# A four-layer graph network: stationary weights in layer 0, row tables made in its loop, fixed order in layer 1, layer 2's tables beside layer 1's lists

## The chip, the cores and the metric

The kernel runs on one core of a Trainium2 chip. The metric is the device time in microseconds; lower is better. PE is the matrix engine (PEld its weight load), DVE the vector engine, ACT the engine of activation functions, POOL the general engine, which here issues the gathers, and SP the engine that issues plain transfers.

## The reference, cut to what matters

B = 8 batches, N = 2048 nodes, D = 64 features; `adj` is 2048 x 2048 with about eight edges a row. Four layers follow each other, each `x = layernorm(x + layer(x, adj))`:

```
layer 0: h = LN((x*nw + nb + x) @ W)
         e = leaky_relu(s1[:, :, None] + s2[:, None, :]); att = softmax(where(adj, e, -big))
         layer = elu(att @ h + h)
layer 1: feat = softplus(x*w0/sqrt(2) + b0); p = exp(feat*wa + ba)       (per feature)
         layer = (A @ (p*feat)) / (A @ p)
layer 2: layer = LN(relu(x @ W_self + b + (A @ x / deg) @ W_neigh + b'))
layer 3: four attention heads over adj, an output product, a second attention, LN
```

`A` is `adj > 0`. The factor `exp(ba)` falls out of layer 1's quotient.

## The kernel before

The nodes are 16 tiles (NT) of 128. A first stage reads `adj`, builds for each tile a list of its edges (five blocks of 128 list places for each of two groups of 64 nodes: GS = 5, NG = 2), the selection matrices `Sel`, `SelT`, and for the first DENSE = 8 tiles the transposed matrix `ET`. It also makes layer 0's `H` and its table `htab0` in DRAM.

A tile's neighbours can be summed in two ways. *By list*: ten gathers (`gather`, L204, an indirect transfer that POOL issues) fetch the neighbours' rows from a table in DRAM, one row per list place, and PE multiplies them by the selection matrices. *By matrix*: PE multiplies `ET` with the rows of all 16 tiles, which must be in SBUF, split into three bf16 pieces (`hi`, `mid`, `lo`).

Layer 0 (L435 to L535) is by list for all tiles, in an order written out by hand (`manual_schedule`: each engine gets its instructions in the order of the Python calls). Step k issues the gathers of tile k+1 (`fetch`), makes the edge weights of tile k (`weights`), divides tile k-1, combines tile k-2 with `H`, multiplies tile k's gathered rows by the weights on DVE and sums them on PE (`weigh`, L476 and L482), then activates tile k-2 and normalises tiles k-3.

Layer 1 (L543 to L692) first makes the rows `p` and `p*feat` of four tiles at a time (`make_rows`, L580 to L597), stores them in the table `rtab` and splits them into the pieces `R` for the matrix way; beside this PE sums matrix tiles 0 to 2 (`FIRST`). When the table is whole, the gathers for tiles 15 to 8 begin, three groups of list blocks a tile (`quads`; four, four and two gathers of 4 KB rows), spread between the steps of matrix tiles 3 to 7. `finish` (L614 to L617) divides and adds to `X`; each pair of tiles is then normalised. A scheduler sets the engines' order here.

Layer 2 (L776 to L1000) turns each tile of `X` and multiplies it by both weight matrices (L805 to L825), stores `ytab`, splits the product into `Y` and keeps `S`. Then, in a fixed order, steps of matrix tiles 0 to 7 and groups of list tiles 15 to 8 (`quads`) alternate; LATE and EARLY say how many matrix steps stand before the first and after the last group. `chain` normalises finished tiles, and `show` copies them on POOL (L908) and stores `xtab`, from which layer 3 gathers.

## Time and profile before

| | us |
|---|---|
| median of 9 runs | 1765.13 (1761.21 to 1769.31) |
| the profiled execution | 1767.85 |
| its span | 1765.7 |
| first gather of layer 0 | 186.1 |
| first weights of layer 0's loop (L461), last | 201.5, 401.1 |
| first gather of layer 1, of layer 2, of layer 3 | 530.8, 749.6, 923.2 |

The profile is one execution. A window's busy time tells how full an engine was in it, not which engine set the pace; the chain of waits and the idle time before an instruction tell that. Instructions of one engine that do not depend on each other overlap a little: DVE's products of 512 elements show 0.69 us each and start 0.60 us apart.

### The profile page before, as it was taken

To read this page: it belongs to the slowest core of one execution; us is meant where nothing else is said; L and a number is where in the kernel's file an instruction comes from. 1 tells how busy PE (TensorE), PEld (TensorE's weight loads), DVE (VectorE), ACT (ScalarE), POOL (GpSimd) and SP (SyncE) were. 2 spreads that over 40 slices of the span, in tenths; PEclk is the share of its full clock that TensorE was granted. 3 is DMA by queue.
4 is the path that set the end of the run, shared out by engine and by line. 5 is a ranking of instruction groups with operands and counts; after the bars stand their busy time and mean duration, and the time that the engine had idled before them with its cause. 6 is when DMAs were issued, how large, how long until landed. Compare 5 with 4: busy or idle time off the path is not lost.

```text
span 1765.7 us, 38671 instructions
## 1 busy us (share of the span) xinstructions
PE 1392.7 (79%) x15264; PEld 956.7 (54%) x15264; DVE 1198.3 (68%) x2931; ACT 932.0 (53%) x1943; POOL 870.8 (49%) x820
## 2 busy tenths in 40 slices
PE   4673354552789996898829999999999986999993
PEld 3663232331233333632217877777777775878783
DVE  5889479996666564765764666666666654787787
ACT  5763244545952232544655656656656533577674
POOL 0000577670665551666525454554554516677761
PEclk9655567666799998999968999999999987999997
DMA  6451576660226982266514555554555427687771
GB/s 187 164 173 42 167 202 192 190 200 17 95 96 241 329 309 87 95 177 187 168 51 124 146 143 141 154 154 130 154 150 155 137 69 228 180 234 219 211 214 45
DMA packets 154135, 280.64 MB, mean 159 GB/s; under 512 B 64892, under 2 KB 91452, under 8 KB 151868
## 3 DMA queue, kind: packets, MB, share of 16 engines
q0 software_dynamic: 56320, 189.44, 35.5%
q1 hardware_dynamic: 80986, 84.45, 16.3%
q10 hardware_dynamic: 16640, 4.20, 1.0%
q8 instruction: 123, 2.02, 0.5%
q14 instruction: 66, 0.54, 0.1%
HBM read 237.60 MB, written 40.42 MB: 157 GB/s over the span
## 4 chain that ended last, share of the span: by engine, by line
PE 43%; DVE 13%; ACT 6%; issue 4%; POOL 2%; DMA 1%; DVEq 0%; SPq 0%; ACTq 0%; POOLq 0%
PE pscore L1081 8%; PE pa L605 6%; PE po L1103 5%; PE pt L1068 4%; PE pscore L1044 4%; PE pa L660 3%; PE ps L1385 2%; PE po L1424 2%; PE py L812 2%; DVE z L1156 2%; PE pt L1362 1%; ACT z L849 1%; PE pa L982 1%; PE pscore L1166 1%; POOL hs L204 1%
## 5 line engine op out<-in xcount | busy, mean ns | idle before, releaser
L204 POOL DMA_INDIRECT hs<-htab,src x160 | 153.2, 957 | 240.4 <-PE pe L455 181.5
L204 POOL DMA_INDIRECT xs<-xtab,src x160 | 207.0, 1294 | 113.9 <-PE po L1103 63.9
L1087 DVE SCALAR_TENSOR_TENSOR w<-w,Sel 128x640 f32<-128x640 f32 (+2 forms) x160 | 153.3, 958 | 135.1 <-ACT w L1084 133.9
L605 PE MATMUL pa<-R,ET 128*128 128x512 bf16 x768 | 178.6, 389 | 51.6 <-POOL R L593 34.6
L204 POOL DMA_INDIRECT hs<-ktab,src x160 | 158.1, 988 | 61.8 <-issue 34.5
L1081 PE MATMUL pscore<-U,xsT 64*128 64x80 f32 (+2 forms) x2560 | 182.7, 282 | 0.0
L1081 PEld LDWEIGHTS pscore<-U,xsT 64*128 64x128 f32 x2560 | 157.5, 189 | 43.5 <-ACT xsT L1070 22.7
L170 ACT ACTIVATE X<-X,ln_m,ln_r 128x64 f32<-128x64 f32 x256 | 87.2, 428 | 144.8 <-DVE ln_m L162 144.8
L605 PEld LDWEIGHTS <-ET 128*128 128x128 fp8e4 x768 | 74.6, 100 | 163.5 <-issue 83.0
L1070 ACT COPY xsT<-pt 128x512 f32<-128x512 f32 x160 | 93.7, 586 | 103.6 <-PE pt L1068 103.6
L1084 ACT ACTIVATE w<-pscore 128x640 f32<-128x640 f32 (+2 forms) x160 | 119.6, 747 | 46.8 <-PE pscore L1081 44.9
L1103 PE MATMUL po<-w,xs 128*64 128x88 f32 (+2 forms) x3072 | 139.6, 237 | 0.7 <-DVE w L1087 0.7
L1068 PE MATMUL pt<-ident,xs 128*128 128x128 f32 x640 | 106.8, 290 | 33.9 <-DMA xs<-xtab,src 33.2
L1103 PEld LDWEIGHTS po<-w,xs 128*64 128x64 f32 x3072 | 114.0, 137 | 15.3 <-DVE w L1087 0.9
L204 POOL DMA_INDIRECT rs<-rtab,src x80 | 75.9, 949 | 62.7 <-PE pa L660 43.1
L614 DVE RECIPROCAL rec<-pa 128x256 f32<-128x256 f32 x32 | 54.2, 1731 | 64.3 <-PE pa L660 38.5
L1385 PE MATMUL ps<-U,hsT 128*128 128x64 f32 x768 | 95.5, 271 | 1.5 <-ACT hsT L1363 1.5
L1385 PEld LDWEIGHTS ps<-U,hsT 128*128 128x128 f32 x768 | 94.2, 195 | 1.9 <-ACT hsT L1363 1.7
L1068 PEld LDWEIGHTS pt<-ident,xs 128*128 128x128 f32 x640 | 68.3, 142 | 48.7 <-DMA xs<-xtab,src 33.4
L476 DVE TENSOR_TENSOR hs<-hs,w 128x1024 f32<-128x1024 f32 x80 | 91.9, 1214 | 3.2 <-ACT w L465 3.2
L1472 ACT ACTIVATE z<-z,ln_m,ln_r 128x64 f32<-128x64 f32 x240 | 83.5, 431 | 15.3 <-DVE ln_m L1460 15.3
L982 PE MATMUL pa<-Y,ET 128*128 128x512 bf16 x384 | 89.9, 383 | 0.0
(636 smaller groups left out, 3077.0 us busy)
## 6 DMA issues: line engine op xcount, KB each, us to landing
at<-in_adj SPq DMA_DIRECT2D x16, 1024.0 KB
R<-itab SPq DMA_DIRECT2D x60, 256.0 KB
rtab<-r SPq DMA_DIRECT2D x16, 512.0 KB
ptab<-hp SPq DMA_DIRECT2D x16, 384.0 KB
hi<-ptab SPq DMA_DIRECT2D x16, 384.0 KB
ktab<-hb SPq DMA_DIRECT2D x16, 260.0 KB
X<-in_x ACTq DMA_DIRECT2D x16, 256.0 KB
htab<-H SPq DMA_DIRECT2D x16, 256.0 KB
```

What stands on the lines that cost most here:

```text
L170: nc.scalar.activation(v[:, b], v[:, b], AF.Identity, scale=rstd[:, k:k + 1], bias=nmr[:, k:k + 1])
L204: nc.gpsimd.indirect_dma_start(out=dst, out_offset=None, in_=table[:, :], in_offset=bass.IndirectOffsetOnAxis(ap=src[:, it, s, g:g + 1], a ...
L476: nc.vector.tensor_tensor(wx, wx, along(w[:, own].rearrange("p g b -> p (g b)")), ALU.mult)
L605: nc.tensor.matmul(po[h].rearrange("p a f -> p (a f)"), ET[:, jt, it * P:(it + 1) * P], R[:, jt, q, h].rearrange("p a f -> p (a f)"), star ...
L982: nc.tensor.matmul(sums[it], ET[:, jt, it * P:(it + 1) * P], Y[:, jt, q].rearrange("p a n -> p (a n)"), start=(jt == 0 and q == 0), stop=( ...
L1068: nc.tensor.transpose(pt[:, p], xss[k][:, p * P:(p + 1) * P], ident)
L1070: nc.scalar.copy(xsTs[k], pt)
L1081: nc.tensor.matmul(pscore[:, k_, f0:f0 + HN * ni].rearrange("p (h i) -> p h i", i=ni), xsT[half, p], Us[it][half, p, :, i0:i0 + ni], start ...
L1084: nc.scalar.activation(w.rearrange("p k a h i -> p k (a h i)"), pscore[:, :, 0:NP * HN * ni], AF.Exp)
L1087: nc.vector.scalar_tensor_tensor(wt, wt, 3.0e38, edge, op0=ALU.min, op1=ALU.mult)
L1103: nc.tensor.matmul(po[half, p, :, a - blk * GB:b - blk * GB], xs[:, f0:f0 + D], w[:, k_, p, :, a - WINDOWS[s][0]:b - WINDOWS[s][0]], start ...
L1385: nc.tensor.matmul(pscore[:, g, 2 * p:2 * p + 2], hsT[:, g, p], U[:, p, :, node_block(g, k)], start=False, stop=(p == NP - 1))
```

## The change

Six parts: the matrix holds seven tiles instead of eight (layer 2 uses seven by matrix and nine by list, layer 1 six and ten). In layer 0 the edge weights become the stationary operand: DVE spreads `Sel` times the weight into `W`, and PE multiplies `W` by the gathered rows, which carry the score and a column of ones (E0 = 66 columns a batch), so that the denominators come from the same products. The loop also makes layer 1's rows and stores them in `rtab`, a few steps behind; six tiles' rows remain for a block of their own after the loop. Layer 1 has a fixed order, reads its rows back from `rtab` and splits them there. Its last six list groups stand beside layer 2's turning and products, whose pieces move from POOL to ACT and DVE. Layer 2's LATE and EARLY become 10 and 4. The parts of layer 3 are as before.

```diff
-    DENSE = 8
+    DENSE = 7
...
+    E0 = D + 2
+    htab0 = dram.tile([N + 1, B * E0], F32, name="htab0")
...
+    H = wp.tile([P, NT, B, E0], F32, name="H")
+    nc.gpsimd.memset(H[:, :, :, 1], 1.0)
...
     def fetch(it):
-        hs = wk.tile([P, GS * NG, B, D], F32, name="hs")
+        hs = [wk.tile([P, GS, B, E0], F32, name="hs", bufs=5) for _ in range(NG)]
...
     def weights(it):
...
+        nc.vector.scalar_tensor_tensor(wm, wm, 0.2, wm, op0=ALU.mult, op1=ALU.max)
+        nc.scalar.activation(pe[:, 1], wm, AF.Exp)
     def weigh(it):
...
+        for g in range(NG):
+            W = wk.tile([P, NQ, B, GB], F32, name="W", bufs=3)
+            for k in range(GN // GB):
...
+                nc.vector.tensor_tensor(W[:, of[0]:of[-1] + 1], Sel[:, it, g, of[0]:of[-1] + 1].unsqueeze(2).to_broadcast(shape),
+                                        pe[:, 1, g, ss[0]:ss[-1] + 1].unsqueeze(3).to_broadcast(shape), ALU.mult)
+            for n in range(NQ // 2):
+                for t in range(B):
+                    j, b = divmod(t, HB)
+                    for q in (n, n + NQ // 2):
+                        s, k = QS[q]
+                        nc.tensor.matmul(pv[node_block(g, k), j, b], W[:, q, t], hs[g][:, s, t, 1:], start=(n == 0 and b == 0),
+                                         stop=(n == NQ // 2 - 1 and b == HB - 1))
...
     def normalise(it):
...
+        nc.scalar.activation(f, X[:, it], AF.Exp, scale=w0, bias=bb)
+    def soften(t0):
+        for t in (t0, t0 + 1):
+            nc.scalar.activation(fs[t], fs[t], AF.Ln, bias=ones_col)
+    def exponentials(it):
+        nc.scalar.activation(rs[it][:, :, 0], rs[it][:, :, 1], AF.Exp)
+    def logits(it, exp=True):
...
+        nc.vector.tensor_tensor(e, fs[it].rearrange("p (h b) d -> p h b d", h=2), over(wa, e.shape), ALU.mult)
+        if exp:
+            exponentials(it)
+    def row_out(it):
+        r = rs.pop(it)
+        nc.vector.tensor_tensor(r[:, :, 1], fs.pop(it).rearrange("p (h b) d -> p h (b d)", h=2), r[:, :, 0], ALU.mult)
+        nc.sync.dma_start(rtab[it * P:(it + 1) * P, :], r.rearrange("p h a n -> p (h a n)"))
...
-            if k % 2 == 0 and k >= 4:
-                normalise(k - 3)
+                if k % 2 == 0 and k < NT - 2:
+                    soften(k - 4)
+            if k % 2 and 5 <= k < NT - 1:
+                logits(k - 5)
+                logits(k - 4)
+            if k % 2 == 0 and k >= 6:
+                row_out(k - 6)
+                row_out(k - 5)
...
+    def load_rows(jt):
...
+            nc.sync.dma_start(rfs[jt], rtab[jt * P:(jt + 1) * P, :])
+    def pieces(jt):
...
+            nc.scalar.copy(hi, rf)
+            nc.vector.tensor_tensor(rf, rf, hi, ALU.subtract)
+            nc.scalar.copy(mid, rf)
+            nc.vector.tensor_tensor(lo, rf, mid, ALU.subtract)
...
+    with tc.manual_schedule(engines=engines):
+        load_rows(0)
+        load_rows(1)
+        soften(NT - 6)
+        combine(NT - 2)
+        normalise(NT - 4)
+        activate(NT - 2)
+        divide(NT - 1)
+        combine(NT - 1)
+        activate(NT - 1)
+        normalise(NT - 3)
+        soften(NT - 4)
+        normalise(NT - 2)
+        normalise(NT - 1)
+        soften(NT - 2)
+        for t in range(NT - 6, NT - 2):
+            logits(t, exp=False)
+        for t in (NT - 2, NT - 1):
+            logits(t)
+        for t in (NT - 2, NT - 1):
+            row_out(t)
+        for t in range(NT - 6, NT - 2):
+            exponentials(t)
+            row_out(t)
...
+    gk = l1.enter_context(tc.tile_pool(name="l1g", bufs=6, reuse_waits="tile"))
...
+    IN_FLIGHT = 6
...
+    def add_edges(n):
...
+        fetch(len(rss.pop(n)))
+    steps = [(it, jt) for jt in range(NT) for it in range(FIRST)] + [(it, jt) for it in range(FIRST, DENSE1) for jt in range(NT)]
+    AMID, LATE = 24, 6
...
+            if k < NT * FIRST and it == 0:
+                pieces(jt + 2)
+                load_rows(jt + 4)
+            add_rows(it, jt)
+            if jt == NT - 1:
+                finish(it)
+            due()
+            if k >= LATE and n < AMID and (k - LATE) * AMID >= n * (len(steps) - LATE):
+                add_edges(n)
+                n += 1
...
+    def products(t):
...
+        nc.scalar.copy(y, py[:, :, 1])
+        nc.sync.dma_start(ytab[t * P:(t + 1) * P, :], y.rearrange("p a n -> p (a n)"))
+        nc.scalar.copy(hi, y)
...
+        nc.vector.tensor_tensor(rest, py[:, :, 1], hi, ALU.subtract)
+        nc.scalar.copy(mid, rest)
+        nc.vector.tensor_tensor(lo, rest, mid, ALU.subtract)
+        nc.vector.tensor_tensor(X[:, t], X[:, t], over(b2, [P, B, D]), ALU.add)
+    with tc.manual_schedule(engines=engines):
+        shown, count = [], 0
+        while count < NT:
+            if n < len(quads):
+                add_edges(n)
+                n += 1
+            due()
+            due()
...
+            for _ in range(1 if n % 2 else 2):
+                if normal:
+                    t = normal.pop(0)
+                    turn_x(t)
+                    shown.append(t)
+                if count < len(shown) - 1 or (count < len(shown) and not normal):
+                    products(shown[count])
+                    count += 1
...
-        LATE, EARLY = 18, 10
+        LATE, EARLY = 10, 4
```

Here FIRST = 3 and DENSE1 = 6: layer 1's first 48 steps give each row tile to three sums. `finish` puts a pair's statistics and its normalising into a queue `later`, from which `due` takes one part at a time; `normal` holds the tiles that may be turned. After the 96 matrix steps, PSUM has one pair of sum tiles left for the six remaining groups.

## The prediction

> **What bounds the kernel now.** I read the windows first, cut where a stage's first or last gather stands (columns: window, its length, then busy time of PE, PEld, DVE, ACT, POOL, the granted clock, DMA share, GB/s).
>
> ```profile
> 186.10:401.10 215.00, 112.21 (x868) 66.21 (x868) 170.01 (x331) 90.77 (x279) 153.18 (x160) 0.69 0.68 196
> 401.10:444.20 43.10, 5.69 (x48) 2.91 (x49) 27.78 (x76) 26.91 (x68) 0.00 (x0) 0.60 0.01 2
> 444.20:530.70 86.50, 67.70 (x275) 28.27 (x275) 58.12 (x46) 62.01 (x71) 57.16 (x32) 0.90 0.25 97
> 530.70:677.70 147.00, 147.00 (x844) 53.96 (x847) 84.58 (x208) 36.55 (x104) 75.90 (x80) 1.00 0.80 286
> 677.70:700.90 23.20, 8.25 (x46) 3.79 (x38) 17.10 (x62) 11.25 (x34) 1.55 (x12) 0.76 0.09 21
> 700.90:749.60 48.70, 42.75 (x206) 34.58 (x207) 34.00 (x51) 25.70 (x47) 30.63 (x32) 0.94 0.24 88
> 749.60:876.30 126.70, 112.12 (x519) 38.22 (x516) 78.03 (x284) 65.70 (x175) 81.77 (x88) 0.93 0.63 180
> 876.30:923.20 46.90, 16.87 (x104) 6.82 (x103) 33.35 (x128) 24.17 (x69) 10.72 (x16) 0.73 0.19 54
> ```
>
> Layer 0's loop is row one; the seam to layer 1 is rows two and three (130 us without a gather, because layer 1's table must be whole before one may start); layer 1 is PE throughout (147.00 of 147.00); rows five and six are the seam to layer 2; layer 2 is row seven, its tail row eight. Layer 3 starts at 923.2 and is not touched. Second, the timeline of POOL (start, busy, instruction, idle before it):
>
> ```profile
> 268.82 0.95 POOL L204 DMA_INDIRECT hs<-htab,src  x1 [0.30 <-issue]
> 270.08 0.96 POOL L204 DMA_INDIRECT hs<-htab,src  x1 [0.30 <-issue]
> 530.77 0.98 POOL L204 DMA_INDIRECT rs<-rtab,src  x1
> 749.61 1.00 POOL L204 DMA_INDIRECT rs<-ytab,src  x1 [0.15 <-DMA AT<-in_L_gnn_bh]
> 852.24 0.96 POOL L204 DMA_INDIRECT rs<-ytab,src  x1 [0.30 <-issue]
> 858.48 0.70 POOL L908 COPY Xo<-X 128x504 f32<-128x504 f32 x1 [5.28 <-issue]
> 861.12 0.61 POOL L908 COPY Xo<-X 128x504 f32<-128x504 f32 x1 [1.95 <-ACT X L849]
> 861.87 0.98 POOL L204 DMA_INDIRECT rs<-ytab,src  x1
> ```
>
> A gather costs POOL 1.26 us (0.96 busy, 0.30 between), so ten make 12.6 us a tile. Layer 0 takes (401.1-201.5)/15 = 13.3 us a tile, with DVE busy 45 of every 50 us: both are near the limit. Layer 2's 80 gathers need 101 us and took 126.7; most of the rest is POOL standing at copies like those of 858 and 861. Third, prices: a timeline line, two pieces of the chain, groups (total, mean ns) and the gather's landing.
>
> ```profile
> 1516.20 1.12 PE L1424 MATMUL po<-hs,w 128*32 128x65 f32 x32
> 548.10 1.85 PE pa L660 x16
> 549.96 3.99 PE pa L605 x18
> L1397 DVE TENSOR_TENSOR w<-Sel,w_mid 128x512 f32<-128x512 fp8e4 x16 | 11.1, 691 | 6.9 <-ACT w_mid L1375 6.9
> L583 ACT ACT_TABLE_LOAD x9 | 11.5, 1283 | 0.2
> L614 DVE RECIPROCAL rec<-pa 128x256 f32<-128x256 f32 x32 | 54.2, 1731 | 64.3 <-PE pa L660 38.5
> ...
> rs<-rtab,src POOLq DMA_INDIRECT x80, 6.0
> ```
>
> **Layer 0's loop.** Removed per tile: five products hs\*w (1.15 us each back to back), one sum, one exponential, the self_ copy, 24 long matmuls. Added: four W products of 768 elements; the trace has that form at 512 (L1397, 0.69) and 1024-element tensor products at 1.21, so 0.96 each, 0.9 back to back. 96 matmuls of 65 columns on 32-column weights: layer 3 has this shape, 32 instructions in 1.05 us between starts, 33 ns each; two per matmul give 6.3 us at full clock, 9 at the 0.69 seen here. Layer 1's row work comes in: exp 0.80, ln 0.72, exp 0.63 on ACT, two products on DVE, two table loads of 1.28 per two tiles. Per two tiles DVE has W 7.0, combine 4.0, activate 2.6, stats 4.1, the row products 3.7 (six and four of 0.6 to 0.69) and small ones 0.7: 22.1; plus two waits of about 1.5 for ACT (exp(k) queues behind normalise, ln and the table load): 25.2. ACT has divide 5.0, normalise 5.5, loads 2.6, the row work 4.3, selTf and the exps 3.0: 20.4. POOL needs 25.1, so POOL and the DVE-ACT chain tie. Gathers may run half a tile further ahead (five half-tile buffers for two whole ones), so the 2.2 us that POOL now waits at 265.05 for PE goes. A gathered row grows from 2048 to 2112 bytes; what costs is the issue, so I add nothing. Ten of the sixteen rtab stores (512 KB) go out during this loop, on SP's queue, which holds nothing else then; the DMA share of 0.68 has room for 5 MB. I take 12.6 us a tile: last weights at 201.5+15x12.6 = 390, plus 2 for slips, 392 (now 401.1). Bounds: 390 if only POOL counts; 407 at 13.7, if the chain or PE does.
>
> **Trainium skill against trace.** "ScalarE: Activation LUTs", section "What ACT_TABLE_LOAD costs", adds a drain of about 1.38 us to every 1.28 us load and says to batch by set; the new loop does the opposite. In the trace the exponential before a load ends at 437.96, the load starts at 437.98 and ln at 439.28: no drain is seen. By the page, ACT would sum to 23.2 us per two tiles and the chain to 28, and the last weights would come near 406.
>
> **Order of layer 0's end.** Six tiles' rows are still open when the last weights are made. In the built order ACT has two extra ln and table pairs ahead of the last exp, so it comes 3 us late: 395. Then, in instruction order: W 3.7; combine 13, activate and stats to +10; combine 14, its exp, activate to +14; divide 15, combine 15 among the first table pieces (1.2 each on DVE, 1.0 on ACT) to +23; stats 14/15 and normalising to +31; three table loads, exp, ln to +38; six exps 3.4, last product +42.5; store landed +48. First layer 1 gather: 443 (now 530.8). Bounds 45 to 53.
>
> **Layer 1.** R is now read back from the table (16 loads of 512 KB) and split by ACT and DVE: 2.1 and 2.4 us per tile, under PE's 4.0 for three accumulations. PE has done seven steps before the lists. The first group needs four gathers, 3.8 us of issue and 6.0 to land: 453. Then 89 steps at 1.33 (3.99/3) = 118.4 and 24 groups at 1.85 = 44.4: 163. In flight are 6 gathers, not 8: every second group of a tile waits for two gathers issued when the first ended, 0.65+6.0 after it, while PE has 5.0 us of matrix work, 1.5 us a tile for 8 tiles: 12. End 628. Bounds of that stall: none, since the present stage shows PE never waiting, to 25 if each group waits.
>
> **The seam with layer 2's tables.** Now 72 us (677.7 to 749.6) with PE at 2.72 a tile. POOL's two pieces go to ACT and DVE, and both queues are fixed: mid(n) on ACT, then lo, X, S, rest on DVE (0.60 each back to back, rest 0.69), then mid(n+1) 0.62. That loop is 3.2 us a tile, 51 for 16. Ahead of it 18.5: finish of tiles 8 and 5 (two reciprocals of 1.7 and four adds of 0.42 each, 5.0), stats, the normalising of 8 and 9 (5.4, in front of ACT's copies), first pieces. Inside: two more finishes 10, stats 4, small work 1, two normalisings that hold ACT 10. With the last store landing 3.8, and 2.3 us of work behind it: 96. First layer 2 gather 724. Bounds 84 (PE's 2.72) to 104 (every hand-over late).
>
> *Small parts.* In the list stage one transposed tile less and three small copies less are hidden by DVE (47 of 50 us busy between 100 and 150); the column of ones is one POOL memset before POOL has any gather. The layer 1 constants (eight small instructions, 1.4 us at 429 to 430) move there too. Wsn and the biases are loaded only when PE has left R: six short loads on SP and a memset on POOL, under the 18.5 us; 16 loads for layer 3 now stand between the ytab stores, at 0.3 to 0.6 us each against 3.2 us a store: hidden, or 6 us if POOL's memsets before them are late.
>
> **Layer 2** has nine list tiles: 90 gathers, 113 us, and the same 25 us at the copies: 138 (now 126.7), bounds 130 to 148. One matrix tile less frees 48 matmuls of PE, 10.6 us, which saves nothing, as POOL sets the pace. Only six matrix steps instead of 13 follow the last list: tail 42 (now 46.9). Layer 3 starts at 724+138+42 = 904 instead of 923: 19 us earlier. The profiled execution took 1767.85 with a span of 1765.7; the median is 1765.13. Forecast 1765-19 = **1746**.
>
> **Rivals.** *More comes through*: PE paces the seam (84) and the list stalls vanish; another 24 us less, 1722. For it: the present seam hides just these waits; against: the pieces leave POOL. *The order's end wins nothing in the loop*: DVE-ACT-PE at 13.7 a tile, +15 and some seam waits: 1764. For it: 25.2 against 25.1. *Slower*: layer 1 becomes a DMA stage. To the 24th group 86 gathers (45 MB) and 14 loads (7.3 MB) must come in; at the 286 GB/s of its present row that is 183 us, what I sum from PE plus stalls; the two kinds queue on the same 16 engines, and at 235 GB/s (the stretch 531 to 560) it is 223: 40 more, 1786. It decides below 258 GB/s, where the gain is used up. Against it: 322 GB/s between 560 and 600.
>
> **Numbers.** Forecast 0.50 (own range 1730 to 1762), more 0.22, nothing in the loop 0.12, slower 0.16. About 0.2% is what a measurement of this kernel tells from no change. Faster: 0.47+0.22+0.04 = 0.73; slower 0.15+0.05+0.02 = 0.22; same 0.05. Range 1712 to 1778.
>
> **What would show it.** Gathers of layer 0 at 1.26 us without gaps; first rtab gather near 443; PE waits on rs in every second group; ACT and DVE alternating at 3.2 us in the seam; first ytab gather near 724, first xtab gather near 904. Wrong if the rtab gather comes after 460, the seam exceeds 105, or PE idles over 25 us in layer 1.

## The result, and the profile after

The changed kernel takes 1775.48 us (median of 10 runs) where the kernel before, on the same chip, takes 1764.45 (31 runs): a ratio of 1.0058, 95% interval 1.0047 to 1.0069. It is slower by 0.6%; forecast was 1746. The ratios here and below leave out single runs that took far longer than the others of their kernel (of these ten, one at 2067.71 us).

The profiled execution took 1769.86 us, its span is 1768.1. The windows again (columns as before: window, length, busy time of PE, PEld, DVE, ACT, POOL, granted clock, DMA share, GB/s), cut at layer 0's loop, its end, layer 1's stretch with matrix steps, the seam, layer 2, its tail:

```profile
187.50:397.90 210.40, 138.44 (x3009) 133.80 (x3011) 141.53 (x340) 120.01 (x296) 155.86 (x160) 0.73 0.77 228
397.90:454.80 56.90, 22.60 (x260) 13.18 (x254) 39.30 (x93) 38.99 (x68) 0.01 (x1) 0.72 0.32 117
454.80:653.45 198.65, 178.41 (x918) 62.18 (x918) 112.49 (x201) 56.22 (x115) 88.07 (x87) 0.97 0.74 253
653.45:751.10 97.65, 63.98 (x309) 39.37 (x309) 66.98 (x156) 52.14 (x112) 14.86 (x26) 0.86 0.40 134
751.10:890.60 139.50, 125.73 (x537) 39.19 (x535) 90.03 (x328) 75.21 (x204) 92.23 (x100) 0.98 0.65 184
890.60:927.80 37.20, 11.47 (x62) 4.05 (x62) 25.10 (x90) 14.61 (x42) 10.10 (x16) 0.68 0.22 59
```

The 130 us from layer 0's last weights to layer 1's first gather have become 57; against that, layer 1 was 147 us and is now 199, the seam was 72 and is 98, layer 2 was 127 and is 139.5. (The kernel before has its last matrix steps behind the cut at 677.7. Cut at their end, 685.1, as in the changed kernel, its layer 1 is 154 us and its seam 65.) The table sets the points of the trace beside the forecast.

| point, us from the span's start | before | forecast | changed | changed minus forecast, stage by stage |
|---|---|---|---|---|
| last weights of layer 0 | 401.1 | 392 | 397.7 | |
| first gather of layer 1 | 530.8 | 443 | 454.8 | +11.8 |
| layer 1's window ends (in the changed kernel: last matrix step) | 677.7 | 628 | 653.45 | +13.65 (198.65 against 185) |
| first gather of layer 2 | 749.6 | 724 | 751.1 | +1.65 |
| last gather of layer 2 | 876.3 | 862 | 890.6 | +1.5 |
| first gather of layer 3 | 923.2 | 904 | 927.8 | -4.8 |

Forecast was 19 us less at the last point; the misses add up to 23.8, and the point is 4.6 later than before. Layer 3 took 842.5 before and 840.3 now.

POOL's timeline (start, busy, instruction, idle before it) and two rows of groups (total, mean ns, then idle time and its releaser) answer to the prices:

```profile
389.63 0.96 POOL L204 DMA_INDIRECT hs<-htab,src  x1 [0.30 <-issue]
390.89 0.95 POOL L204 DMA_INDIRECT hs<-htab,src  x1 [0.30 <-issue]
```

```profile
L494 PE MATMUL po<-hs,W 128*32 128x65 f32 x2865 | 113.9, 259 | 40.6 <-DVE W L487 23.4 <-issue 17.2
L487 DVE TENSOR_TENSOR W<-Sel,pe 128x768 f32<-128x768 fp8e4 x60 | 53.1, 948 | 9.1 <-ACT pe L475 9.1
```

Layer 0's gathers follow each other every 1.26 us to the end, but for eleven that come 1.33 to 1.80 us after the one before (160 gathers in 203.3 us, 12.8 a tile). A W product costs 0.95 us, forecast at 0.96.

Layer 1 shows what is new. PE's timeline, first around the second list group of tile 14, then around the first group of tile 12:

```profile
493.24 1.05 PE L724 MATMUL pa<-rs,self__4783 128*32 128x512 f32 x4
495.11 1.04 PE L724 MATMUL pa<-rs,self__4783 128*32 128x512 f32 x2 [0.82 <-DMA rs<-rtab,src]
497.09 1.90 PE L724 MATMUL pa<-rs,self__4783 128*32 128x512 f32 x10 [0.93 <-DMA rs<-rtab,src]
...
526.76 1.92 PE L724 MATMUL pa<-rs,self__4851 128*32 128x512 f32 x16
528.61 5.35 PE L626 MATMUL pa<-R,ET 128*128 128x512 bf16 x24
536.39 1.06 PE L724 MATMUL pa<-rs,self__5003 128*32 128x512 f32 x8 [2.43 <-issue]
539.03 1.94 PE L724 MATMUL pa<-rs,self__5003 128*32 128x512 f32 x8 [1.57 <-DVE X L680]
```

A group whose rows are there takes 1.86 us up to the next matrix step; the group at 493.24 takes 5.68, in three pieces, as the rows of its last gathers come in. The group at 536.39 waits for something else: `X` of the finish, that is, for the pair of PSUM tiles of the list tile before it. DVE and ACT at that place:

```profile
520.29 5.41 ACT L170 ACTIVATE X<-X,ln_m,ln_r 128x64 f32<-128x64 f32 x16
525.60 1.03 ACT L611 CAST R<-rf 128x1024 bf16<-128x1024 f32 x1
```

```profile
526.66 1.23 DVE L612 TENSOR_TENSOR rf<-rf,R 128x1024 f32<-128x1024 f32 x1 [5.02 <-ACT R L611]
...
532.48 1.23 DVE L614 TENSOR_TENSOR R<-rf,R 128x1024 bf16<-128x1024 f32 x1 [1.11 <-ACT R L613]
533.62 1.75 DVE L677 RECIPROCAL rec<-pa 128x256 f32<-128x256 f32 x1
```

PE had finished the list tile at 528.6, but its finish begins on DVE at 533.62: ahead of it in DVE's fixed order are two sets of pieces, and these waited for ACT, which was normalising a pair of tiles. Three of the four PSUM pairs belong to the matrix tiles 0 to 2 at this time; the lists have one.

### The profile page after: what moved, and what is told of

The parts are those of the page before. It is cut to its first block, busy times and chain, and to the rows that moved or that the text cites. A ratio compares the mean times of both kernels' runs of the same rounds, so it can differ in the third digit from the quotient of the medians.

```text
span 1768.1 us, 43032 instructions
## 1 busy us (share of the span) xinstructions
PE 1422.6 (80%) x17432; PEld 1015.5 (57%) x17432; DVE 1169.7 (66%) x2945; ACT 940.6 (53%) x1926; POOL 821.1 (46%) x787
## 4 chain that ended last, share of the span: by engine, by line
PE 40%; DVE 23%; ACT 10%; issue 7%; DMA 6%; POOL 4%; DVEq 0%; SPq 0%; POOLq 0%; ACTq 0%
PE pscore L1173 8%; PE po L1195 5%; PE pt L1160 4%; PE pscore L1136 4%; PE pa L626 4%; POOL hs L204 3%; DMA rs<-rtab,src 3%; PE pa L724 2%; PE ps L1477 2%; ACT X L170 2%; PE po L1516 2%; DVE z L1248 2%; DVE W L487 2%; DMA hs<-htab,src 2%; PE pt L1454 1%
## 5 line engine op out<-in xcount | busy, mean ns | idle before, releaser
L204 POOL DMA_INDIRECT rs<-rtab,src x100 | 101.3, 1013 | 200.7 <-PE pa L724 116.1
L494 PE MATMUL po<-hs,W 128*32 128x65 f32 x3072 | 122.4, 260 | 48.8 <-DVE W L487 23.4
L626 PE MATMUL pa<-R,ET 128*128 128x512 bf16 x576 | 134.1, 387 | 26.5 <-ACT R L611 18.1
L494 PEld LDWEIGHTS po<-hs,W 128*32 128x32 f32 x3072 | 118.2, 137 | 51.7 <-DVE W L487 25.4
L1195 PE MATMUL po<-w,xs 128*64 128x88 f32 (+2 forms) x3072 | 139.5, 237 | 0.7 <-DVE w L1179 0.7
L170 ACT ACTIVATE X<-X,ln_m,ln_r 128x64 f32<-128x64 f32 x240 | 81.9, 428 | 94.7 <-DVE ln_m L162 94.7
L204 POOL DMA_INDIRECT rs<-ytab,src x90 | 87.1, 968 | 73.1 <-DMA ytab<-y 47.0
L626 PEld LDWEIGHTS <-ET 128*128 128x128 fp8e4 x576 | 55.0, 99 | 114.0 <-issue 50.9
```

The lines of the kernel that those rows point to most:

```text
L170: nc.scalar.activation(v[:, b], v[:, b], AF.Identity, scale=rstd[:, k:k + 1], bias=nmr[:, k:k + 1])
L204: nc.gpsimd.indirect_dma_start(out=dst, out_offset=None, in_=table[:, :], in_offset=bass.IndirectOffsetOnAxis(ap=src[:, it, s, g:g + 1], a ...
L494: nc.tensor.matmul(pv[node_block(g, k), j, b], W[:, q, t], hs[g][:, s, t, 1:], start=(n == 0 and b == 0), stop=(n == NQ // 2 - 1 and b == ...
L626: nc.tensor.matmul(po[h].rearrange("p a f -> p (a f)"), ET[:, jt, it * P:(it + 1) * P], R[jt][:, q, h].rearrange("p a f -> p (a f)"), star ...
L1195: nc.tensor.matmul(po[half, p, :, a - blk * GB:b - blk * GB], xs[:, f0:f0 + D], w[:, k_, p, :, a - WINDOWS[s][0]:b - WINDOWS[s][0]], start ...
```

## The experiments

All edits are made to the changed kernel. The ratio is to the kernel before on the same chip. Eight of the eighteen kernels ran on two chips like the first (the kernel before takes 1765.7 there); ten ran on three chips where it takes 1868 to 1870, and are compared with one another and by distances within the trace. "Stretch" is the time from layer 1's first gather to the end of its last matrix step (198.65 and, in a second profile of the changed kernel, 201.2), "seam" the time from there to layer 2's first gather (97.65 and 98.4).

**Eight gathers in flight.**

```diff
-            rfs[jt] = ra.tile([P, 2 * BD], F32, name="rf", bufs=2)
+            rfs[jt] = [ra.tile([P, BD], F32, name="rf", bufs=3) for _ in range(2)]
...
-    gk = l1.enter_context(tc.tile_pool(name="l1g", bufs=6, reuse_waits="tile"))
+    gk = l1.enter_context(tc.tile_pool(name="l1g", bufs=8, reuse_waits="tile"))
...
-    IN_FLIGHT = 6
+    IN_FLIGHT = 8
```

> Layer 1 with eight of its gathers in flight instead of six (the room comes from loading R's rows in halves and from two buffers for self_ instead of three). In the changed kernel PE waited 15.9 us for gathers between 454 and 660, nearly all in the second group of a tile, and the first list group to the last matrix step took 188 us (465.5 to 653.4). Theory A, too few gathers in flight: those waits fall below 4 us, the stretch to 172-178, the first ytab gather comes near 739 instead of 751, and the time falls by 10 to 14 us, a ratio of 0.997 to 1.000 to the kernel before. Rival C, layer 1 is at what the DMA engines give: a gather then lands 8 us after its issue instead of 5.2 to 6.1, PE still waits 12 us or more, the stretch stays above 184, ratio 1.004 to 1.007.

1767.34 us, ratio 1.0003 (0.999 to 1.0015). The waits for gathers after the first group are gone: the eight second groups of the tiles together last 15.1 us, in the changed kernel 32.2, in the kernel before 14.9. But the stretch is 196.9, 1.8 less than in the changed kernel. (The 172 to 178 of the expectation count from the first list group, 10 to 16 us less than now. Counted from the end of that group it is 183.1 here and 186.1 in the changed kernel, 3 less.) PE's timeline of this kernel:

```profile
529.38 3.41 PE L627 MATMUL pa<-R,ET 128*128 128x512 bf16 x15
533.43 2.40 PE L627 MATMUL pa<-R,ET 128*128 128x512 bf16 x9 [0.63 <-ACT R L614]
543.21 1.94 PE L725 MATMUL pa<-rs,self__5246 128*32 128x512 f32 x8 [7.39 <-issue]
545.85 1.93 PE L725 MATMUL pa<-rs,self__5246 128*32 128x512 f32 x8 [0.70 <-DVE X L681]
```

The stop for the PSUM pair has grown from 4.0 us (2.43 and 1.57) to 8.1, with another of 4.2 at 510: PE ends the list tile at 529.4, the finish stands behind four more sets of half pieces and begins at 540.43. Theory A has its cause, and in the stretch a second wait takes most of what it should give. The median is 8 us below the changed kernel's; of that, the two profiles show 2.8 up to layer 3.

**The seam's subtractions on POOL.**

```diff
-        nc.vector.tensor_tensor(rest, py[:, :, 1], hi, ALU.subtract)
+        nc.gpsimd.tensor_tensor(rest, y, hi, ALU.subtract)
...
-        nc.vector.tensor_tensor(lo, rest, mid, ALU.subtract)
+        nc.gpsimd.tensor_tensor(lo, rest, mid, ALU.subtract)
```

> In the seam to layer 2 the two subtractions that make the pieces of Y go back from DVE to POOL. Theory E, the loop between ACT and DVE paces the seam (3.2 us a tile seen): the last matrix step of layer 1 to the first ytab gather falls from 97.7 us to 84-88, ratio 0.997 to 1.000. Rival: PE with its one pair of PSUM tiles, the six last list groups and the normalising in front of ACT's copies set the length: it stays above 94, ratio 1.004 to 1.007. Third way: POOL, at about 1 us a subtraction and with the last gathers of layer 1 ahead of them, is the slower one: above 100.

1780.05 us, ratio 1.0074 (1.0056 to 1.0092); the seam lasts 104.4 us. POOL takes 1.61 and 1.16 us where DVE took 0.69, and the loop goes through ACT as before, 3.96 us a tile instead of 3.18. The third way came true: the loop goes over the hand-overs from hi to rest and from rest to mid, whoever subtracts, and POOL is the slower one.

**Layer 2's LATE and EARLY as before.** `LATE, EARLY = 18, 10`.

> Layer 2's lists begin after 18 matrix steps and end 10 steps before the last (the numbers of the kernel before) instead of 10 and 4; all else as changed. My sum gave the new numbers a gain in the tail: it was 46.9 us before and is 37.2 now. If they are what shortened it, the tail from the last ytab gather to the first xtab gather goes back to 43-47 and the last ytab gather stays at 139.5 us after the first (POOL's pace), ratio 1.008 to 1.011. Rival: the tail is short because of one matrix tile less, and stays at 37 to 39, ratio 1.004 to 1.007.

1780.74 us, ratio 1.0076 (1.0057 to 1.0096). Layer 2 and its tail in this kernel:

```profile
753.24:887.76 134.52, 118.09 (x491) 36.58 (x498) 82.29 (x289) 66.23 (x176) 91.28 (x98) 0.96 0.66 189
887.76:934.13 46.37, 18.09 (x98) 7.55 (x99) 33.28 (x128) 24.04 (x69) 10.44 (x16) 0.70 0.20 55
```

The tail goes from 37.2 back to 46.4 us, as the first theory has it, but the gathers end 5 us sooner; together 180.9 against 176.7. The new numbers are worth 4 us.

**Rows not loaded again.**

```diff
-            rfs[jt] = ra.tile([P, 2 * BD], F32, name="rf", bufs=2)
-            nc.sync.dma_start(rfs[jt], rtab[jt * P:(jt + 1) * P, :])
+            if jt == 0:
+                rfs[0] = ra.tile([P, 2 * BD], F32, name="rf", bufs=1)
+                nc.sync.dma_start(rfs[0], rtab[0:P, :])
```

> R's pieces are all made from one tile of rows, loaded once: the 15 other loads of 512 KB are left out, so layer 1 has the wrong rows in its matrix part; the same work on ACT, DVE and PE. Rival C, the loads take DMA time from the gathers: PE's waits for gathers in layer 1 fall from 15.9 us below 6, the gathers land in under 5 us up to 560, the stretch from the first list group to the last matrix step falls from 188 to 176 or less, ratio 0.998 to 1.001. Theory A, the gathers' own latency with six in flight: most of the waits are after the last load (560) and stay; 3 to 5 us less in all, ratio 1.003 to 1.005.

1774.38 us, ratio 1.0045 (1.003 to 1.006). The stretch is 198.6 us and the second groups last 32.0, both as in the changed kernel, though the engines moved 223 GB/s instead of 253. Rival C falls: the transfers did not set the pace, their rate followed from it.

**The seam one tile apart.**

```diff
         nc.vector.tensor_tensor(rest, py[:, :, 1], hi, ALU.subtract)
+        rests[t] = rest
+
+    def last_pieces(t):
+        mid, lo = Y[t][:, 1], Y[t][:, 2]
+        rest = rests.pop(t)
         nc.scalar.copy(mid, rest)
...
                     products(shown[count])
+                    if count:
+                        last_pieces(shown[count - 1])
                     count += 1
+        last_pieces(shown[-1])
```

> In the seam mid, lo and the sum of X are made one tile later (behind y, hi, S and rest of the next tile), so that ACT and DVE no longer wait for each other within a tile; nothing else. Theory E, the hand-overs between ACT and DVE pace the seam at 3.18 us a tile: without them ACT's four copies (2.2) and DVE's four (2.4) do, 2.4 to 2.6 us a tile, and the last matrix step of layer 1 to the first ytab gather falls from 97.7 us to 85-89, ratio 0.998 to 1.001. Rival: the finishes, statistics and normalisings that stand in both queues set the length, the loop only fills between them: 93 to 97, ratio 1.003 to 1.006.

On a chip where the kernel before takes 1868: 1929.58 us, ratio 1.0308 (1.0276 to 1.034), seam 90.65. The ratio is far from every theory; it had to do with the chip, and the kernel ran once more below.

**Buffers meant to come free earlier**, same chip as the last.

```diff
-        for h in range(2):
-            for (s, g), rs in rss[n].items():
-                for k, _, _ in blocks_of(s):
+        for (s, g), rs in rss[n].items():
+            for k, _, _ in blocks_of(s):
+                for h in range(2):
```

> Layer 1's list groups run their two halves of a gathered tile one after the other (the gather is the outer loop), so that a group's first buffers come free after a quarter of its matmuls, and six in flight are refilled about 1.4 us sooner; the same matmuls. Theory A: PE's waits for gathers after the first list group (8.6 us in the changed kernel, 8.6 = 15.9 - 7.3) fall below 3, layer 1 gets 5 to 8 us shorter, ratio 1.001 to 1.004. Rival B, the one PSUM pair that the lists have while three matrix tiles hold the others: it takes the saved time back in waits for DVE's finish (10.8 us now, 15 with eight in flight): less than 3 us shorter, ratio 1.004 to 1.006.

1933.65 us, ratio 1.0328 (1.0298 to 1.0357); stretch 202.8 us, second groups 32.0: nothing gained. In a group whose rows are all there the premise was wrong: POOL's next gather starts when the group has ended (the group from 581.25 to 583.44, the gather at 583.43), not after its first quarter. In second groups, which wait for rows, buffers did come free earlier: in the one from 588.73 to 592.91 the next gather starts at 590.90, also 2.2 us after the group's first matmul. In the changed kernel it starts only as such a group ends (518.49 to 522.77, the gather at 522.27). That made these groups no shorter.

**Normalising held back**, same chip.

```diff
-            due()
+            if k >= NT * FIRST:
+                due()
```

> Statistics and normalising of layer 1's finished tiles stand behind the 48 steps in which pieces are made, instead of among them. Theory B, the 5.4 us of normalising on ACT at 520 delay the pieces, these the finish of a list tile on DVE, this the PSUM pair of the next: the stop of PE at 534 to 541 (2.43 and 1.57 us) goes, waits for X and issue in layer 1 fall from 10.8 to 5-7, layer 1 is 4 us shorter, ratio 1.002 to 1.005 unless the seam gives it back. Rival A: the gathers set the pace there (none is under way at 540 only because PE is late): under 2 us shorter, ratio 1.005 to 1.007.

1925.58 us, ratio 1.0315 (1.0287 to 1.0343), 8 us below the run before it, whose interval overlaps with this one. What tells them apart is the trace. Its stretch beside that of the kernel above (first line: normalising held back; second, in a fence of its own: loop order only):

```profile
525.63:718.39 192.76, 178.66 (x918) 62.21 (x918) 112.49 (x201) 56.41 (x115) 87.93 (x87) 0.97 0.75 261
```

```profile
524.50:727.31 202.81, 187.30 (x918) 66.98 (x918) 111.57 (x200) 56.60 (x115) 86.68 (x87) 0.95 0.72 248
```

Ten us less; every first group of tiles 14 to 8 takes 1.86 us, where one takes 6.2 in the kernel beside it (4.5 in the changed kernel) at the stop. Theory B holds, and was priced too low (4).

**Ten row stores out of the loop**, same chip.

```diff
+    for t in range(NT - 6):
+        nc.sync.dma_start(rtab[t * P:(t + 1) * P, :].rearrange("p (k n) -> p k n", n=128), filler.unsqueeze(1).to_broadcast([P, 2 * BD // 128, 128]))
...
+        if it >= NT - 6:
+            nc.sync.dma_start(rtab[it * P:(it + 1) * P, :], r.rearrange("p h a n -> p (h a n)"))
```

> The ten stores of 512 KB that layer 0's loop sends to layer 1's table are left out; that part of the table is filled with ones before layer 0 (so layer 1 has the wrong rows there). The gathers of layer 0's last tile landed 6.8 us after their last issue, 2.7 in the kernel before, and DVE's waits for gathered rows went from 28 to 49 us. Theory D, the stores share the DMA engines with the gathers: the rows land within 4 us, the last weights come 3 us sooner, first rtab gather near 452 against 454.8, ratio 1.003 to 1.005. Rival: the stores had room and the wait comes of the larger rows and the gathers being nearer together: no sooner than 1 us, ratio 1.005 to 1.007.

1954.92 us, ratio 1.0461 (1.0429 to 1.0494), of which the filling is about 25 us (first gather at 211.4). Layer 0's gathers last 269.9 us, in the three kernels beside it 269.5 to 271.9; DVE's waits for rows are 24.6 us against 25.2. On this chip the stores cost nothing.

**The changed kernel again, and three versions**, on a chip where the kernel before takes 1765.7.

> The changed kernel itself, as the yardstick of the runs beside it. The last four runs took 1908 to 1955 us where the kernel before took 1868: in them layer 0's loop lasted 269 us instead of 203 (PE's 192 small matmuls a tile with gaps on PE that nothing else released), although none of them touches it. If that belongs to the chip on which a run is made, the kernel here is either at 1.004 to 1.008 with layer 0's gathers over 201-205 us, or at 1.030 to 1.036 with 265-275 us. If it belonged to those edits, it is at 1.004 to 1.008 wherever the kernel before takes 1868.

1776.18 us, ratio 1.0063 (1.0044 to 1.0082), layer 0's gathers 203.4 us. The next kernel, at 1.0308 above, is at 1.0011 here: so the 1.03 does not belong to the edits. Stretch 201.2, seam 98.4, first gather of layer 3 at 929.0.

> The same kernel as in the run on the seam before, beside the changed kernel. Theory E (hand-overs between ACT and DVE): first ytab gather 8 to 12 us sooner after the last matrix step of layer 1 than in the changed kernel, time 8 to 12 us below it. Rival (finishes and normalising set the length): under 4 us.

1767.68 us, ratio 1.0011 (0.9998 to 1.0025), seam 89.6 (98.4 beside it). ACT's timeline in the changed kernel and in this one:

```profile
740.86 0.62 ACT L799 CAST Y<-rest 128x512 bf16<-128x512 f32 x1 [0.94 <-DVE rest L798]
741.39 0.58 ACT L128 COPY xT<-pt 128x512 f32<-128x512 f32 x1
741.87 0.59 ACT L792 COPY y<-py 128x512 f32<-128x512 f32 x1
742.48 0.62 ACT L794 CAST Y<-y 128x512 bf16<-128x512 f32 x1
744.04 0.62 ACT L799 CAST Y<-rest 128x512 bf16<-128x512 f32 x1 [0.94 <-DVE rest L798]
```

```profile
735.34 0.61 ACT L804 CAST Y<-rest 128x512 bf16<-128x512 f32 x1
735.86 0.58 ACT L128 COPY xT<-pt 128x512 f32<-128x512 f32 x1
736.37 0.59 ACT L792 COPY y<-py 128x512 f32<-128x512 f32 x1
736.99 0.62 ACT L794 CAST Y<-y 128x512 bf16<-128x512 f32 x1
737.51 0.61 ACT L804 CAST Y<-rest 128x512 bf16<-128x512 f32 x1
```

From mid to mid it takes 3.18 us in the first, with 0.94 spent waiting for rest, and 2.17 in the second, with none in these lines. Theory E holds.

> Layer 1 with seven gathers in flight (what fits without loading rows in halves) and the gather as outer loop of a group. Theory A: PE's waits for gathers after the first group below 2 us (8.6 in the changed kernel), first ytab gather 5 to 8 us sooner, time 5 to 8 us below the changed kernel. Rival B: the waits move to the PSUM pair that DVE's finish frees; under 3 us.

(Loop order as above, `bufs=7` and `IN_FLIGHT = 7`.) 1764.51 us, ratio 0.9989 (0.9975 to 1.0003): 11.7 us below the changed kernel, more than either theory gave. The stretch is 194.6, the second groups last 18.8 us; as the loop order alone did nothing (on another chip, with six in flight), this is put down to the seventh buffer; seven without the loop order was not tried. 9.5 us of waits for the PSUM pair remain (4.2, 3.1 and 2.2).

> Seven in flight, the gather as outer loop, normalising held back behind the pieces, the seam one tile apart. If the causes are separate, their gains add: 8 (gathers) + 4 (PSUM pair) + 10 (seam) = 22 us below the changed kernel, a ratio of about 0.993 where the changed kernel is at 1.006. If they hide one another, 10 to 14 us below, ratio 0.998 to 1.000.

1748.76 us, ratio 0.9903 (0.9886 to 0.992): 27.4 us below the changed kernel; the profiles show 22 of it up to layer 3 (first gather at 907.1 against 929.0). The expected sum was 22: the causes are separate and their gains add. This version is faster than both kernels. Its stretch and seam, and PE's three groups of tile 9:

```profile
452.45:640.99 188.54, 173.66 (x900) 64.56 (x918) 111.48 (x200) 55.07 (x112) 89.69 (x88) 0.97 0.77 268
640.99:729.13 88.14, 64.92 (x305) 40.35 (x306) 66.17 (x156) 52.91 (x115) 14.18 (x25) 0.83 0.42 144
```

```profile
601.85 1.94 PE L724 MATMUL pa<-rs,self__5460 128*32 128x512 f32 x16
609.01 1.94 PE L724 MATMUL pa<-rs,self__5460 128*32 128x512 f32 x16
614.88 1.94 PE L724 MATMUL pa<-rs,self__5460 128*32 128x512 f32 x16
```

All three groups of this tile run through. Not every stop is gone: three second groups still last 2.6 to 3.5 us, and the first groups of tiles 13 and 12 last 4.5. The stretch is 12.7 us shorter than in the changed kernel on the same chip, the seam 10.3.

**What was still open.** Six more kernels ran on two chips where the kernel before takes 1868 to 1870.

> The kernel with layer 1's normalising held back until the pieces are made, beside the kernel before once more (its first run had no yardstick). By difference it gave 7 us when it stood beside the other two edits. Theory B (normalising delays the pieces, these the finish, this the PSUM pair): the last matrix step of layer 1 ends 4 to 7 us sooner than the changed kernel's 653 to 654, ratio 1.001 to 1.004. Rival: it only pays where gathers are no longer waited for; alone under 2 us, ratio 1.005 to 1.007.

> Layer 1's normalising held back until the pieces are made, alone (both runs so far fell on chips where the kernel before takes 1868). Theory B: the last matrix step of layer 1 ends 4 to 7 us sooner after the first gather of layer 1 than the changed kernel's 198.6 and 201.2 us, ratio 1.001 to 1.004 where the kernel before takes 1765. Rival: alone under 2 us, 1.005 to 1.007.

1926.52 us, ratio 1.0309 (1.0281 to 1.0338), and 1929.75, ratio 1.0314 (1.0286 to 1.0341). The stretches are 192.5 and 195.5 us. On the same two chips the kernels without ten stores (below), which leave layer 1's normalising where it is, have 199.9 and 201.4; on the chip of the first run it was 192.8 against 201.1 to 203.0 in three. So it is worth 6 to 10 us of the stretch by itself on such chips; with the other edits, on the first kind, 194.6 against 188.5 gives 6. Its ratio alone, where the kernel before takes 1765, was not measured.

> As in the first run of this kernel, layer 0's loop leaves out ten of the sixteen stores to layer 1's table, which is filled with ones there (about 25 us of work ahead of layer 0, so only distances within the trace are read). Theory D, the stores delay the last gathered rows: from the last gather of layer 0 to the first of layer 1 it takes 58 to 60 us instead of 63.9, and DVE's waits for gathered rows fall from 37 us to 25 or less between the first gather and 390. Rival, the rows are late for the size and the rate of the gathers: 63 us or more, waits above 33.

> Ten of the sixteen stores to layer 1's table left out and filled with ones ahead of layer 0. On the chips where the kernel before takes 1868 it changed nothing: DVE's waits for gathered rows 24 against 25 us, the last rows 12 us after their issue with stores and without. Theory D: where PE doesn't pace the loop, the stores take the time: waits fall from 49 to 30 us or less (28 in the kernel before), the last weights come within 4.5 us of the last gather's issue instead of 6.8. Rival: the gathers nearer together do it: waits above 42, last weights 6 us or more after.

1961.52 us, ratio 1.0504 (1.0477 to 1.053), and 1964.81, ratio 1.0508 (1.048 to 1.0537). From layer 0's last gather to layer 1's first it takes 67.7 and 68.6 us; 69.6 and 68.4 in the kernels beside them that store. The waits for rows are 24.1 and 24.5 us against 25.1 and 24.9. The stores cost at most 2 us there; where PE does not pace the loop it stays untried.

> The kernel before itself: ratio 1. Its first profile was 3.4 us above its median, and ended layer 2 at 923.2. If the distance of the medians (10 to 11 us) is all made before layer 3, this profile has its first xtab gather at 918 to 921 with a span near 1762, and the changed kernel's 927.8 and 929.0 are 8 to 10 later. If the kernel before varies mostly in layer 3, the gather is at 922 to 924 again.

1871.22 us, ratio 1.0021 (0.9998 to 1.0043). On this chip it can't tell where the 10 us between the medians lie, but it shows what the slower chips do to the kernel before (last section).

> The four edits together (0.9903) and layer 1's normalising shared by ACT and DVE (8 instructions each of a pair's 16). If the 5.4 us that ACT's copies stand behind it in the seam are on the path (three times, at 653, 668 and 707), 2.7 us come off each time: the seam 6 to 8 us shorter, ratio 0.985 to 0.987. If DVE's 1.9 us for its half lie on the path in their place: 0 to 3 us, ratio 0.989 to 0.991.

```diff
+            if c % 2:
+                nc.scalar.activation(v, v, AF.Identity, scale=rstd[:, c:c + 1], bias=nmr[:, c:c + 1])
+            else:
+                nc.vector.tensor_scalar(v, v, rstd[:, c:c + 1], nmr[:, c:c + 1], op0=ALU.mult, op1=ALU.add)
```

1909.91 us, ratio 1.0207 (1.0175 to 1.0238), 20 us below the kernel with the normalising held back on the same chip. The seam lasts 84.2 us, 88.1 in the version without this edit (another chip): about half of what was hoped.

## Why the prediction was wrong, step by step

Two steps failed: the pace of layer 0's loop, and the sum of layer 1, in which one stall was too small and a second stood at nothing. The order between the two layers added to the first.

**Layer 0's loop.** The step that failed is "I take 12.6 us a tile ... plus 2 for slips, 392". I had POOL and the chain of DVE and ACT tie, at 25.1 and 25.2 us for two tiles. POOL never waited, but took 12.8 us a tile, and its last gather starts at 390.9. The last weights start 6.8 us later (3.8 in the kernel before, counted alike). The expectations of the runs without stores read this as rows that land late. DVE's timeline says otherwise:

```profile
388.97 3.55 DVE L487 TENSOR_TENSOR W<-Sel,pe 128x768 f32<-128x768 fp8e4 x4 [1.46 <-ACT pe L475]
395.20 0.69 DVE L522 SCALAR_TENSOR_TENSOR X<-e,X 128x512 f32<-128x512 f32 x1 [2.68 <-ACT e L517]
...
396.54 1.28 DVE L560 TENSOR_TENSOR r<-f,r 128x512 f32<-128x512 f32 x2
397.74 0.35 DVE L473 TENSOR_TENSOR wm<-pe,hs 128x40 f32<-128x40 f32 x2
```

The weights (L473) follow the instruction ahead of them without idle time; what DVE waits for here is ACT, whose queue has two table loads in it (389.16 and 393.29). DVE's last wait for rows ends at 343.15. In the run with seven in flight, whose layer 0 is the same, these gathers land 3.9 us after their issue (3.7 in the kernel before), so the last rows were there near 395, by estimate. From 343 on the chain is the slower one: the last four tiles take 13.8 us each (weights at 342.38 and 397.74), where the sum had 12.6. In the two tiles from 332.05 to 359.01, 26.96 us, DVE is busy for 21.25, forecast 22.1, and waits 1.45 for ACT and 3.02 for PE's products, a wait that my sum had at nothing. The three runs without stores, all on slower chips where PE paces the loop, could not have shown this; no run shortened the chain where the kernel before takes 1765, so this is read from the trace and not tested.

**The order's end.** I had 48 us from the last exponential to the first gather, bounds 45 to 53; it took 52.8 (402.0 to 454.8). The start was 7 us late (weights 5.7, ACT 1.3). ACT's queue shows most of the rest:

```profile
414.14 0.58 ACT L517 ACTIVATE e<-z 128x512 f32<-128x512 f32 x1 [5.12 <-DVE z L515]
418.56 1.04 ACT L611 CAST R<-rf 128x1024 bf16<-128x1024 f32 x1 [3.83 <-DMA rf<-rtab]
```

The first table piece stands in the fixed order before its rows have come from the table; ACT waits 3.83 us for them, DVE's piece behind it 2.45, and only then DVE combines tile 15. The last product ends at 447.65, 45.6 us after the exponential instead of 42.5, and from there to the first gather it takes 7.1 instead of 5.5. Together +11.8.

**Table loads.** By the Trainium skill ("ScalarE: Activation LUTs", section "What ACT_TABLE_LOAD costs") a drain of some 1.38 us would stand beside each load. The pair ahead of the last exponential shows none: load at 398.70 (1.28 us), ln at 399.99, load at 400.73, exponential at 402.02. The row was right to use. (The rule to batch by set, which the prediction names with that section, stands in the page's next one, "Table sets: the hidden batching unit".)

**Layer 1** holds the largest miss, 198.65 against 185. The term "every second group of a tile waits ... 1.5 us a tile for 8 tiles: 12" named the right wait and was too small: the second groups lasted 32.2 us, 17.3 more than in the kernel before, 2.2 a tile; that is 5.3 of the miss of 13.65. The run with eight in flight brought them to 15.1. A term was missing altogether: with fixed order and one PSUM pair for the lists, DVE's finish is on PE's path, and whatever stands ahead of it on DVE and ACT too. It cost 6.2 us of idle time here (2.4, 1.6 and 2.2 around tile 12) and 6 to 10 in all by the runs that moved the normalising. I had checked pieces (2.4 us a tile) against PE's 4.0 as sums per engine, not what the order puts ahead of the finish.

**The seam** was right: 96 forecast, 97.65 measured, with the loop of 3.2 us a tile seen. That it was a choice of order and not a necessity I did not see: one tile of distance takes 8.8 us off.

**Layer 2** was right to 1.5 us; the tail was 4.8 better than forecast.

**The rivals.** The slower one named layer 1 too, by a wrong mechanism. It was to decide below 258 GB/s; 253 were measured, and yet it was not the cause: without the loads the rate falls to 223 and the stretch stays, with most of the waits gone it rises to 268. The rival that wins nothing in the loop had the right chain, DVE, ACT and PE, at 13.7 us a tile; the last four tiles took 13.8. None of the three signs that I had set for "wrong" was met (gather after 460, seam over 105, PE idle over 25 us; PE's idle time in the stretch is 20.2): the gain of 19 us was lost to five small misses, four of one sign. The range, up to 1778, held the time; the likeliest sum and the chance of 0.73 for faster did not. I had treated the misses of the stages as independent; the two large ones have in part one root, a fixed order in which one late piece stops what stands behind it. With the edits against the three waits that the runs found, the same stages give 1748.76. That this is near the 1746 of the sum is in part luck: the first gather of layer 1 still comes 9.5 us later than forecast (452.45), and a seam of 88.1 instead of 96 makes up for most of it.

**What stays open.** The points of the two first profiles account for 4.6 us up to layer 3, the medians differ by 11. The profiled execution of the kernel before was 3.4 us above its median, that of the changed one 5.6 below. The second profile of the changed kernel has its point at 929.0; no second one of the kernel before exists on such a chip.

## What to carry to other kernels

When a scheduler's order is replaced by a fixed one, follow each buffer that the slowest engine needs back to the instruction that frees it, and count what stands ahead of that instruction on its engine: a sum of busy times per engine doesn't show it. A gather that takes 6 us from issue to landing needs as many buffers as are consumed in that time; here a seventh beside the six took away most of the wait. A copy that waits for the other engine's answer within one tile can stand one tile later; here that cost nothing.

## What the runs showed of the hardware that was not expected

The runs fall into two kinds by the chip that they ran on, and the change fares differently on them. (Each of the five chips of the experiments was used at one time only, so that a chip is not told from its time.) Where the kernel before takes 1765 us its layer 0 gathers last 211 us and the changed kernel's 203; where it takes 1868 they last 237, and in the nine runs of changed versions 269.5 to 279. The kernel before loses most in layer 3, which takes 909 us there instead of 842.5. No version came below 1.02 there, the one at 0.9903 with a further edit at 1.0207. Windows of the run with the normalising held back, all within one tile of layer 0's loop:

```profile
290.80:294.50 3.70, 3.60 (x113) 3.33 (x114) 0.27 (x2) 3.67 (x5) 1.39 (x2) 0.97 0.28 82
294.50:300.30 5.80, 2.22 (x33) 1.50 (x32) 0.00 (x0) 0.60 (x2) 3.40 (x4) 0.79 0.72 198
```

and PE's timeline in the second of them:

```profile
294.84 0.37 PE L494 MATMUL po<-hs,W 128*32 128x65 f32 x6 [0.38 <-issue]
...
296.30 0.30 PE L494 MATMUL po<-hs,W 128*32 128x65 f32 x3 [0.39 <-issue]
...
298.47 0.43 PE L494 MATMUL po<-hs,W 128*32 128x65 f32 x4 [1.07 <-issue]
```

PE does 113 of the small matmuls in 3.7 us, and then 33 in 5.8, with gaps of 0.4 to 1.1 us that nothing in the profile ends, while gathers move 198 GB/s (82 in the fast stretch). On the first kind of chip it did 190 in 6.8 us at 248 GB/s. With 192 such matmuls a tile PE paces the loop on the slower chips, and POOL no longer does: DVE waits 113.9 us for PE's products in this run, 6.7 in the changed kernel on the first kind. What the gaps wait for was not found.

A stop of PE can cost more than its idle time. In the fastest version, after a wait of 5.5 us at the start of the seam, 14 matmuls of a list group take 3.63 us, where 16 take 1.94 elsewhere; the granted clock is 0.50 from 646 to 652.5 and 1.00 between 560 and 586:

```profile
560.00:586.00 26.00, 25.74 (x143) 9.92 (x138) 24.31 (x78) 16.11 (x49) 11.38 (x12) 1.00 0.70 227
649.00:652.50 3.50, 3.50 (x14) 0.63 (x14) 3.50 (x23) 0.00 (x0) 0.96 (x1) 0.50 0.00 0
```

The Trainium skill ("TensorE: Matmul & The Clock Gate", Part 1) has the clock fall to half after an idle window of about 3.4 us and rise after a busy one as long; the two rows agree with it: PE stood still from 641.0 to 646.5, and a window of its granted clock from 652.5 to 656 shows 1.00 again. My sum of layer 1 priced every matmul at the full clock.
